# Text keys of the semantic scores copied on chip, and the second entry's scores ahead of slot 0

## The chip, the cores and the metric

The kernel runs on one core of one Trainium2 chip. The metric is the device time of one launch in microseconds. A run is compared by the median of its executions, and one further execution is recorded by the hardware profiler. The views quoted below come from that recorded execution.

## What is computed

Two cross-attention layers follow each other over 16 batch entries of 256 positions and 320 channels, with 20 heads of 16 channels. Both take the same context of 16 x 256 x 512. In layer 0 the first 77 context rows are text and the other 179 are image tokens; in layer 1 the last 4 rows are image tokens. The change touches layer 0 alone, and there the part that the reference writes as

```python
text_probs = softmax(einsum('bqc,bkc->bqk', q, k_text) * scale)   # over all channels, no heads
q_sem = einsum('bqk,bkc->bqc', text_probs, text)
sem = einsum('bqc,bnc->bqn', q_sem, ip) * scale
fused = scores + 0.5 * sem[:, None]                                # scores: per head, q x ip keys
ip_probs = softmax(fused) * spatial_mask
out = (text_out + ip_out) @ Wout + bout + x
```

The text keys `k_text` are thus needed twice: by head, in the attention itself, and over all 320 channels at once, in the semantic scores.

## The kernel before

**Numbers and splitting.** All products are made in a rounded 32-bit format. A value that needs more precision is held as a high part, rounded by ScalarE, and a low part, the difference, made by `halves` (line 148 holds the subtraction, line 147 the copy). A product of two such values takes three matmuls (`prod`, line 205).

**Slots.** Layer 0 is worked through in 80 slots, one for each entry and group of four heads, five groups to an entry; layer 1 follows with 80 more. `slot0(k)` writes one slot's order out by hand: the transposed maxima of slot k+1 (`maxima0`, matmul at line 657, then a copy and four small DMAs at line 661 into rows of `qs`), two rounds of score matmuls for slot k+2 (`score0`, line 649, with VectorE's row maxima at 650 and 651), two rounds of transposed scores for slot k (`turned0`, line 673, with the exponential on ScalarE at 676 and a product with `rs` on GpSimd at 679), the weighted values of slot k-1 (`attend0`, line 709, then `settle0`, lines 720 to 727), and `stacks(k + 4)`, DMAs that lay queries, keys and semantic rows of slot k+4 into `qs` and `ks`. PE's order is exactly the order of these calls. Before slot 0 a hand-written start-up, `begin`, fixes the order on every engine; after it, PE alone is fixed and the other queues are ordered by the compiler's scheduler.

**Tasks.** What an entry or a pair of entries needs besides is a generator with a list of due times in slots; `fill(now)` steps the earliest ones due. Those that matter here:

- `k0` c, the keys of entries 2c and 2c+1 (`keys0`; for pair 0 `keys_first`). It loads the pair's context (`context`, four 256 KB DMAs and four splittings, the low halves on GpSimd where the load is spread over slots), multiplies by the text and the image key weights for each of three blocks of 128 channels, splits the result into `kst`, a ring of two, and writes it to the DRAM tensor `kd` (`keys_out`).
- `q0` b, the queries, kept on chip as `qh` and written to `qd`.
- `m0t` b, the products of text and context rows; `v0` b, the values.
- `s0` b, the semantic scores (`semantic0`), in seven steps: fetch the text keys `kt`; two steps of six matmuls each of `qh` with `kt` (line 571) and their row maxima (573 to 578); exponentials (582); their normalisation (586); transposition (590) and splitting into `tph`; product with `m0t` (599, 600) and the exponential `rs`.

**Text keys.** `kt` lies in the buffer `kb`, of which there is one. For entry 0 `keys_first` fills it by three GpSimd copies from `kst` (line 331). For each of the other 15 entries the first step of `s0` issues two DMAs on SP's queue that read `kd` back, 144 KB each. In layer 1 `image1` uses `kb` for something else.

**The order at the start.** `s0` 1 takes its first step at the end of `begin`, which queues its two DMAs on SP ahead of the maxima of slot 1 and ahead of the context loads of `k0` 1. Its matmuls stand on PE at the end of slot 0, its transposition at the end of slot 1, its last product in slot 2. Because `stacks(5)`, the first of entry 1, needs `tph` of entry 1, slot 1 has no call of `stacks` and slot 2 has two. `s0` 2 fetches its keys in slot 2 and has its matmuls on PE in slot 3.

Of the kernel before, what the change touches and what calls it, by code (L numbers as in the profile page):

```python
# [9 lines left out]
FR = mybir.dt.float32r  # L10
# [7 lines left out]
S = 256  # L18
# [5 lines left out]
T0 = 77  # L24
# [14 lines left out]
LEAD = 4  # L39
# [9 lines left out]
def xattn2(  # L49
# [27 lines left out]
    nc = tc.nc  # L77
    f = lambda ap: ap.bitcast(F32)
    mm = nc.tensor.matmul

    def dma(out, in_):
        nc.sync.dma_start(*(f(ap) if ap.dtype == FR else ap for ap in (out, in_)))
# [11 lines left out]
        return ps.tile([128, 1024], F32, tag="S", name="S", bufs=1).rearrange("p (h t) -> p h t", h=4)  # L94


    words, slots = {"ctb": 1024, "cta": 1024, "raw": 512, "rawc": 512, "kb": 768, "si": 256, "mt": S, "mx": 2, "kst": 4 * S, "rs": 2 * S, "P": 4 * S}, {}

    def buf(tag, shape, dtype=F32, bufs=1, name=None):
        if tag in ("wB", "wD", "vr", "raw"):  # L100
# [108 lines left out]
    def context(b, n, wait=0):  # L209

        tiles, parts = [], []
        for k in range(0, 4, 3 - n):
            src = cT_d[:, b * S : (b + n) * S].rearrange("(k p) t -> p k t", p=128)[:, k : k + 3 - n]
            ct = buf("cta" if n == 1 or k < 2 else "ctb", [128, 2, 512], FR, bufs=SIZES["CTA" if n == 1 or k < 2 else "CTB"], name="ct")
            split = lambda t: t.rearrange("p (k t) -> p k t", t=n * S)
            parts.append((src, split(ct[:, 0]), split(ct[:, 1])))
            tiles.append(ct)
        yield from in_turn(parts, wait, "rawc raw" if b == 2 and n == 2 else "rawc", nc.gpsimd if wait else nc.vector)
        if n == 2:
            return lambda s, k: tiles[k][:, s].rearrange("p (b t) -> p b t", b=2)  # L220
        return lambda s, k: tiles[k // 2][:, s, (k % 2) * S : (k % 2 + 1) * S]
# [68 lines left out]
    def keys_out(d, m, kst, b=slice(None)):  # L290

        rows = slice(m * 128, (m + 1) * 128)
        for r, s in ((slice(0, 2), 0), (slice(2, 3), 1)):
            src = kst[:, s, b].rearrange("p b t -> p (b t)").unsqueeze(1)
            dma(d[r, rows, b].rearrange("r p b t -> p r (b t)"), src.to_broadcast([128, r.stop - r.start, src.shape[2]]))

    def keys0(c):
        if c not in ct0:
            tiles = context(2 * c, 2, 0.25)
            yield next(tiles)  # L300
            get("v0", 2 * c - 1)
            get("m0t", 2 * c - 1)
            ct0[c] = yield from tiles
        ct = ct0[c]
        for m in range(3):
            ms = slice(m * 128, (m + 1) * 128)
            kst = buf("kst", [128, 2, 2, S], FR, bufs=SIZES["KST"])
            for w, lo, hi, a, z in ((wk0, 0, 96, 0, T0), (wki0, T0 - 1, S, T0, S)):
                kp = bank()[:, : 2 * (hi - lo)].rearrange("p (b t) -> p b t", b=2)
                prod(kp, lambda s, k: w(s, k, ms), lambda s, k: ct(s, k)[:, :, lo:hi], 4)  # L310
                halves(kst[:, 0, :, a:z], kst[:, 1, :, a:z], kp[:, :, a - lo : z - lo])
                if a:
                    keys_out(kd[0][c], m, kst)
                yield

    def keys_first():

        ct = ct0[0]
        kst = [buf("kst", [128, 2, 2, S], FR, bufs=SIZES["KST"]) for i in range(2)]
        kst.append(buf("ho", [128, 5 * S], FR)[:, : 4 * S].rearrange("p (s b t) -> p s b t", s=2, b=2))  # L320
        kt = buf("kb", [128, 3, 2, 96], FR, name="kt")
        for w, lo, hi, a, z in ((wk0, 0, 96, 0, 96), (wki0, T0 - 1, S, T0, S)):
            for m in range(3):
                ms = slice(m * 128, (m + 1) * 128)
                kp = bank()[:, : 2 * (hi - lo)].rearrange("p (b t) -> p b t", b=2)
                prod(kp, lambda s, k: w(s, k, ms), lambda s, k: ct(s, k)[:, :, lo:hi], 4)
                halves(kst[m][:, 0, :, a:z], kst[m][:, 1, :, a:z], kp[:, :, a - lo : z - lo])
                if a:
                    keys_out(kd[0][0], m, kst[m], slice(0, 1))
                else:  # L330
                    nc.gpsimd.tensor_copy(kt[:, m], f(kst[m][:, :, 0, :96]))
                yield kt
        for m in range(3):
            keys_out(kd[0][0], m, kst[m], slice(1, 2))
        yield kt

    def values0_(b):
        ct, i = ct0[b // 2], b % 2
# [215 lines left out]
    def semantic0(b):  # L554

        qh, qd = get("q0", b)
        NT = 96
        kt = first_kt[0] if b == 0 else buf("kb", [128, 3, 2, NT], FR, name="kt")
        for s, r in ((0, 0), (1, 2)) if b else ():
            dma(kt[:, :, s], kd[0][b // 2, r].rearrange("(m p) b t -> p m b t", p=128)[:, :, b % 2, :NT])  # L560
        yield
        mh = get("m0t", b)

        tps = []
        for t in range(2):
            sf = bank()
            for k in range(3):
                qt = lambda h: qh[:, h, k, t * 128 : (t + 1) * 128]
                for h in range(2):
                    both = kt[:, k].rearrange("p s n -> p (s n)")  # L570
                    mm(sf[:, : 2 * NT], qt(h), both, start=k + h == 0, stop=k + h == 3)
            sp = buf("sp", [128, T0], bufs=2)
            nc.scalar.copy(sp, sf[:, NT : NT + T0])
            nc.vector.tensor_add(sp, sp, sf[:, :T0])
            mz = buf("mx", [128, 2], bufs=2)
            mx, zs = mz[:, 0:1], mz[:, 1:2]
            nc.vector.tensor_reduce(mx, sp, axis=AX.X, op=ALU.max)
            nc.vector.tensor_scalar_mul(mx, mx, -SCALE)
            tps.append((sp, mx, sp, zs))
            yield  # L580
        for sp, mx, tp, zs in tps:
            nc.scalar.activation(tp, sp, AF.Exp, bias=mx, scale=SCALE, accum_out=zs)
        yield
        for sp, mx, tp, zs in tps:
            nc.vector.reciprocal(zs, zs)
            nc.vector.tensor_scalar_mul(tp, tp, zs)
        yield
        tpp = bank()
        for t in range(2):
            nc.tensor.transpose(tpp[:T0, t * 128 : (t + 1) * 128], tps[t][2], ident)  # L590
        tph = buf("tph", [T0, 2, S], FR, bufs=2)
        nc.scalar.copy(tph[:, 0], tpp[:T0, :S])
        nc.vector.tensor_sub(tph[:, 1], tpp[:T0, :S], f(tph[:, 0]))
        yield

        rs = buf("rs", [128, 2, S], bufs=2)
        rp = bank().rearrange("p (t q) -> p t q", t=2)
        for t in range(2):
            mm(rp[:, t], mh[:, 0, t * 128 : (t + 1) * 128], tph[:, 1], start=True, stop=False)
            mm(rp[:, t], mh[:, 1, t * 128 : (t + 1) * 128], tph[:, 0], start=False, stop=True)  # L600
        nc.scalar.activation(rs, rp, AF.Exp, scale=SCALE)
        yield
        return qd, tph, rs, mh


    QK, P, W, R = {}, {}, {}, {}
# [81 lines left out]
    def slot0(k):  # L688
        if k > 0:
            yield lambda: maxima(k + 1)  # L690
        yield lambda: ahead(k + 2, 0)
        yield lambda: turned0(k, 0)
        yield 0.2
        if k == 2:
            yield lambda: stacks(k + LEAD - 1)
        if k > 0:
            yield lambda: attend0(k - 1)
        yield lambda: ahead(k + 2, 1)
        yield lambda: turned0(k, 1)
        if k != 1:  # L700
            yield lambda: stacks(k + LEAD)
        yield 0.6
        yield 1.0

# [257 lines left out]
    def task(key, times, make, *needs):  # L962
        tasks[key] = [times, 0, make, needs, len(tasks)]
# [38 lines left out]
    def shifted(n, *times):  # L1002

        return [RAMP(n + t) for t in times]

    first_kt, resid0 = [], []

    def first_keys():
        for kt in keys_first():
            if not first_kt:  # L1010
                first_kt.append(kt)
            yield

    FIRST = {"k0": [-1, 0.2, 0.6, 0.6, 1, 1.2, 1.6, 1.6, 2, 2.2, 2.6], "s0": [-1, 0.6, 1, 1.2, 1.6, 1.6, 2.2]}
    for c in range(B // 2):
        n, k = 10 * c, [("k0", c)] if c else []
        task(("k0", c), FIRST["k0"] if c == 1 else shifted(n, -14.4, -13.3, -13, -12.4, -12, -10.8, -10.4, -9.8, -9.4, -8.8, -8.4), (lambda c=c: keys0(c)) if c else first_keys,
             *([("w4", 0)] if c > 1 else []))
        task(("q0", 2 * c), shifted(n, -11.8, -11, -10, -9, -8), lambda b=2 * c: queries0(b))
        task(("q0", 2 * c + 1), shifted(n, -4.4, -4, -3, -2.8, -2), lambda b=2 * c + 1: queries0(b))  # L1020
# [26 lines left out]
    def stacks(k):  # L1047
        if 0 <= k < 2 * NS:
            (stacks0 if k < NS else stacks1)(k)
# [11 lines left out]
    def begin():  # L1061
# [25 lines left out]
        score0(1, 0)  # L1087
        stacks0(3)
        score0(1, 1)
        parts(("s0", 1))  # L1090
        maxima0(1, nc.sync)
        parts(("k0", 1))
        resid0.append(load(xT_d[0], "xc"))
        dma(mk, mk_d)
        dma(bo[:, 0, :], bo0_d)
# [95 lines left out]
```

## Time and profile before

| | |
|---|---|
| median of 3 runs | 1643.64 us (1639.58 to 1647.11) |
| the profiled execution | 1646.73 us, of which 1644.9 us from the first to the last instruction |
| mean granted TensorE clock | 0.972 |
| busy: PE, VectorE, ScalarE, GpSimd | 1539.0, 1197.1, 830.3, 1184.0 us |
| DMA, mean over the span | 150 GB/s |

Layer 0 takes about the first 650 us of the span, at some 8.2 us a slot. Times in the views are microseconds from the start of the span. In the timeline a row is a group of like instructions: start, length, engine, line, operation, output and input tile, shapes, count, and in brackets how long the engine had stood idle before it and what ended that. "PEld" is TensorE's weight load. A row of the stretches gives the length, then the busy time of PE, PEld, DVE, ACT and POOL with counts, the granted TensorE clock, the DMA share and the rate.

### The profile page before, as it was taken

To read this page: it belongs to the slowest core of one execution; us is meant where nothing else is said; L and a number is where in the kernel's file an instruction comes from. 1 tells how busy PE (TensorE), PEld (TensorE's weight loads), DVE (VectorE), ACT (ScalarE), POOL (GpSimd) and SP (SyncE) were. 2 spreads that over 40 slices of the span, in tenths; PEclk is the share of its full clock that TensorE was granted. 3 is DMA by queue.
4 is the path that set the end of the run, shared out by engine and by line. 5 is a ranking of instruction groups with operands and counts; after the bars stand their busy time and mean duration, and the time that the engine had idled before them with its cause. 6 is when DMAs were issued, how large, how long until landed. Compare 5 with 4: busy or idle time off the path is not lost.

```text
span 1644.9 us, 36268 instructions
## 1 busy us (share of the span) xinstructions
PE 1539.0 (94%) x13306; PEld 1239.6 (75%) x13306; DVE 1197.1 (73%) x2404; ACT 830.3 (50%) x1797; POOL 1184.0 (72%) x1131
## 2 busy tenths in 40 slices
PE   7789999999999899689999999999999999999996
PEld 6677878787878787577777777777777777777765
DVE  5467777677666677867777787778777887787685
ACT  5335445445454545435555455545555555555462
POOL 3358787868686867767687767767776787678675
PEclk9799999999999999789999999999999999999998
DMA  7766777777777676565324333343334233423301
GB/s 220 203 207 197 219 202 218 202 210 196 207 198 222 180 213 172 162 198 179 121 86 132 119 104 108 124 127 97 115 118 133 88 123 110 142 82 106 109 26 44
DMA packets 247742, 247.49 MB, mean 150 GB/s; under 512 B 31050, under 2 KB 231468, under 8 KB 247564
## 3 DMA queue, kind: packets, MB, share of 16 engines
q1 hardware_dynamic: 245356, 243.87, 50.1%
q8 instruction: 106, 1.74, 0.5%
q10 hardware_dynamic: 2208, 1.30, 0.3%
q14 instruction: 72, 0.59, 0.1%
HBM read 121.21 MB, written 88.18 MB: 127 GB/s over the span
## 4 chain that ended last, share of the span: by engine, by line
PE 54%; DVE 14%; DMA 10%; POOL 9%; ACT 5%; issue 4%; SPq 2%; ACTq 0%; POOLq 0%; DVEq 0%
PE X L205 16%; PE X L814 10%; PE X L522 7%; PE P L709 5%; POOL wt L805 4%; PE S L649 3%; PE P L823 3%; PE T L673 3%; DMA qs<-qd 3%; PE P L826 3%; PE T L775 2%; DMA qs<-mt 2%; DVE ho L512 2%; DMA kd<-kst 2%; DVE wt L815 2%
## 5 line engine op out<-in xcount | busy, mean ns | idle before, releaser
L679 POOL TENSOR_TENSOR P<-P,rs 128x512 f32<-128x512 f32 x320 | 412.6, 1310 | 171.3 <-ACT P L676 170.9
L805 POOL TENSOR_TENSOR wt<-P,ctb 128x512 f32<-128x512 f32 x320 | 422.4, 1335 | 117.1 <-ACT ctb L804 115.9
L814 PE MATMUL X<-ctb,gm 128*128 128x512 f32 x1120 | 328.8, 412 | 2.5 <-DVE wt L815 2.5
L676 ACT ACTIVATE P<-T 128x512 f32<-128x512 f32 x320 | 176.2, 595 | 234.5 <-PE T L673 118.4
L786 ACT ACTIVATE P<-T 128x512 f32<-128x512 f32 x320 | 174.1, 597 | 142.4 <-PE T L775 121.8
L815 DVE TENSOR_TENSOR wt<-X,wt 128x512 f32<-128x512 f32 x320 | 216.7, 679 | 25.7 <-PE X L814 23.0
L804 ACT ACTIVATE ctb<-P 128x512 fp32r<-128x512 f32 x320 | 195.8, 631 | 74.9 <-PE X L814 63.2
L814 PEld LDWEIGHTS X<-ctb,gm 128*128 128x128 f32 x1120 | 188.8, 188 | 49.4 <-DVE wt L815 5.2
L781 DVE TENSOR_REDUCE mn<-S 128x4 fp32r<-128x1008 f32 x160 | 191.1, 1194 | 0.6 <-PE S L780 0.6
L651 DVE TENSOR_REDUCE mn<-S 128x4 fp32r<-128x716 f32 x160 | 142.6, 891 | 0.0
L673 PE MATMUL T<-qs,ks 127*128 127x256 f32 x640 | 112.6, 296 | 22.9 <-DVE tmp L726 9.8
L649 PE MATMUL S<-ks,qs 125*128 125x256 f32 x640 | 119.1, 310 | 11.2 <-DVE mn L651 3.5
L709 PE MATMUL P<-P,vr 128*32 128x256 f32 x1920 | 128.9, 404 | 0.0
L649 PEld LDWEIGHTS S<-ks,qs 125*128 125x128 f32 x640 | 89.9, 197 | 48.3 <-issue 38.3
L522 PE MATMUL X<-ho,wF 128*128 128x256 f32 x768 | 112.9, 290 | 7.1 <-DVE ho L512 3.0
L894 POOL TENSOR_TENSOR r<-u,rs 128x40 f32<-128x40 f32 (+2 forms) x17 | 108.7, 6393 | 14.8 <-DVE u L891 14.7
L522 PE MATMUL X<-hq,wE 128*128 128x256 f32 x768 | 110.7, 288 | 6.6 <-POOL hq L512 3.1
L673 PEld LDWEIGHTS T<-qs,ks 127*128 127x128 f32 x640 | 93.3, 199 | 28.0 <-DVE tmp L726 11.7
L522 PEld LDWEIGHTS X<-ho,wF 128*128 128x128 f32 x768 | 103.6, 195 | 12.8 <-DVE ho L512 4.7
L522 PEld LDWEIGHTS X<-hq,wE 128*128 128x128 f32 x768 | 102.9, 194 | 11.0 <-POOL hq L512 3.8
L205 PE MATMUL X<-cta,wA 128*128 128x252 f32 (+1 forms) x720 | 100.9, 287 | 7.7 <-ACT wA L147 5.8
L650 DVE TENSOR_REDUCE mn<-S 128x4 fp32r<-128x308 f32 x160 | 74.8, 468 | 44.8 <-PE S L649 44.2
(196 smaller groups left out, 2814.9 us busy)
## 6 DMA issues: line engine op xcount, KB each, us to landing
qd<-q SPq DMA_DIRECT2D x96, 384.0 KB
qs<-tph SPq DMA_DIRECT2D x64, 308.0 KB
kd<-kst SPq DMA_DIRECT2D x73, 256.0 KB
rawc<-in_cT_dram SPq DMA_DIRECT2D x60, 256.0 KB
qs<-qd SPq DMA_DIRECT2D x80, 192.0 KB
ks<-kd SPq DMA_DIRECT2D x80, 192.0 KB
ks<-kd SPq DMA_DIRECT2D x160, 96.0 KB
qs<-qd SPq DMA_DIRECT2D x160, 96.0 KB
```

The source lines that it names most:

```text
L205: last = mm(out, lhs(a, k), rhs(b, k), start=i == 0, stop=i == len(terms) - 1)
L522: mm(pp, w(s, k, slice(m * 128, (m + 1) * 128)), a[:, t], start=i == 0, stop=i == len(terms) - 1)
L649: mm(sp[:, h], Q[: XROW + T0, h, t * 128 : (t + 1) * 128], K[: XROW + T0, h], start=True, stop=True)
L673: mm(st[p][:, j], K[:KS0, 2 * p + j, t * 128 : (t + 1) * 128], Q[:KS0, 2 * p + j], start=True, stop=True)
L676: exp = anchor(nc.scalar.activation(pt, st[p], AF.Exp, scale=SCALE))
L679: anchor(nc.gpsimd.tensor_mul(pt, pt, rs[:, t : t + 1].to_broadcast([128, 2, S])))
L709: mm(pv[32 * s : 32 * s + 32, o : o + S], v[:, vt, h : h + 32], P[k, s // 2][:, t, s % 2], start=vt < 2, stop=vt != 1,)
L781: anchor(nc.vector.tensor_reduce(maxes[k + 2][:, t], sp[:, :, :T1], axis=AX.X, op=ALU.max))
L804: nc.scalar.activation(R[k, u][:, t], P[k, u][:, t], AF.Copy, scale=0.5)
L805: anchor(nc.gpsimd.tensor_sub(W[k, u][:, t], P[k, u][:, t], f(R[k, u][:, t])))
L814: mm(yp, gm[:, gb], R[k, u][:, kt], start=i == 0, stop=i == len(blocks[n]) - 1)
L815: nc.vector.tensor_mul(W[k, u][:, n], yp, W[k, u][:, n])
```

## The change

- `kt` now holds both entries of a pair, 128 x 3 x 2 x 2 x 96 words, and `kb` grows from 768 to 1152 words.
- `keys0` fills it for every pair: after each splitting of a block of text keys, GpSimd copies 2 x 2 x 77 words a partition from `kst` into it. The 30 DMAs from `kd` to `kb` are gone; the first step of `s0` only picks its entry's part. `keys_first` clears the buffer once and copies both entries of pair 0.
- The matmul of line 571 reads two runs of 96 words that no longer lie side by side; its size stays.
- `s0` 1 moves ahead: `begin` makes its fetching step and its twelve matmuls before the maxima of slot 1 and its exponentials and normalisation after them, and its last two steps are due in slot 0 at 0.2 and 0.6. On PE the twelve matmuls therefore stand before the maxima of slot 1, the transposition between the two rounds of slot 0, the last product at slot 0's end.
- With that, `stacks(k + LEAD)` is called in every slot: `stacks(5)` in slot 1 and not in slot 2.
- The low halves of the context of pair 1 are made by VectorE, not GpSimd. They stand in VectorE's queue between the row maxima of slots 2 and 3 and after them.

```diff
@@ context
-        yield from in_turn(parts, wait, "rawc raw" if b == 2 and n == 2 else "rawc", nc.gpsimd if wait else nc.vector)
+        yield from in_turn(parts, wait, "rawc raw" if b == 2 and n == 2 else "rawc", nc.gpsimd if wait and b != 2 else nc.vector)
@@ keys0
         ct = ct0[c]
+        kt = kts[c] = buf("kb", [128, 3, 2, 2, 96], FR, name="kt")
         for m in range(3):
...
                 if a:
                     keys_out(kd[0][c], m, kst)
+                else:
+                    nc.gpsimd.tensor_copy(kt[:, m, :, :, :T0], f(kst[:, :, :, :T0]))
                 yield
@@ keys_first
-        kt = buf("kb", [128, 3, 2, 96], FR, name="kt")
-        for w, lo, hi, a, z in ((wk0, 0, 96, 0, 96), (wki0, T0 - 1, S, T0, S)):
+        kt = kts[0] = buf("kb", [128, 3, 2, 2, 96], FR, name="kt")
+        nc.gpsimd.memset(f(kt), 0.0)
+        for w, lo, hi, a, z in ((wk0, 0, 96, 0, T0), (wki0, T0 - 1, S, T0, S)):
...
-                    nc.gpsimd.tensor_copy(kt[:, m], f(kst[m][:, :, 0, :96]))
+                    nc.gpsimd.tensor_copy(kt[:, m, :, :, :T0], f(kst[m][:, :, :, :T0]))
@@ semantic0
-        kt = first_kt[0] if b == 0 else buf("kb", [128, 3, 2, NT], FR, name="kt")
-        for s, r in ((0, 0), (1, 2)) if b else ():
-            dma(kt[:, :, s], kd[0][b // 2, r].rearrange("(m p) b t -> p m b t", p=128)[:, :, b % 2, :NT])
+        kt = kts[b // 2][:, :, :, b % 2]
...
-                    both = kt[:, k].rearrange("p s n -> p (s n)")
-                    mm(sf[:, : 2 * NT], qt(h), both, start=k + h == 0, stop=k + h == 3)
+                    mm(sf[:, : 2 * NT].rearrange("p (s n) -> p s n", s=2), qt(h), kt[:, k], start=k + h == 0, stop=k + h == 3)
@@ slot0
-        if k == 2:
-            yield lambda: stacks(k + LEAD - 1)
...
-        if k != 1:
-            yield lambda: stacks(k + LEAD)
+        yield lambda: stacks(k + LEAD)
@@ due times of s0 for entry 1
-"s0": [-1, 0.6, 1, 1.2, 1.6, 1.6, 2.2]
+"s0": [-1, -1, -1, -1, -1, 0.2, 0.6]
@@ begin
-        parts(("s0", 1))
+        parts(*[("s0", 1)] * 3)
         maxima0(1, nc.sync)
-        parts(("k0", 1))
+        parts(("s0", 1), ("s0", 1), ("k0", 1))
```

More of the change, by code (lines that the diff above doesn't have):

```diff
@@ L94, in scores @@
         return ps.tile([128, 1024], F32, tag="S", name="S", bufs=1).rearrange("p (h t) -> p h t", h=4)
-    words, slots = {"ctb": 1024, "cta": 1024, "raw": 512, "rawc": 512, "kb": 768, "si": 256, "mt": S, "mx": 2, "kst": 4 * S, "rs": 2 * S, "P": 4 * S}, {}
+    words, slots = {"ctb": 1024, "cta": 1024, "raw": 512, "rawc": 512, "kb": 1152, "si": 256, "mt": S, "mx": 2, "kst": 4 * S, "rs": 2 * S, "P": 4 * S}, {}
     def buf(tag, shape, dtype=F32, bufs=1, name=None):
@@ L295, in keys_out @@
             dma(d[r, rows, b].rearrange("r p b t -> p r (b t)"), src.to_broadcast([128, r.stop - r.start, src.shape[2]]))
+    kts = {}
     def keys0(c):
@@ L330, in keys_first @@
                 else:
-                    nc.gpsimd.tensor_copy(kt[:, m], f(kst[m][:, :, 0, :96]))
-                yield kt
+                    nc.gpsimd.tensor_copy(kt[:, m, :, :, :T0], f(kst[m][:, :, :, :T0]))
+                yield
         for m in range(3):
             keys_out(kd[0][0], m, kst[m], slice(1, 2))
-        yield kt
+        yield
     def values0_(b):
@@ L1004, in shifted @@
         return [RAMP(n + t) for t in times]
[L1006 to L1014, printed above, removed]
+    resid0 = []
+    FIRST = {"k0": [-1, 0.2, 0.6, 0.6, 1, 1.2, 1.6, 1.6, 2, 2.2, 2.6], "s0": [-1, -1, -1, -1, -1, 0.2, 0.6]}
     for c in range(B // 2):
         n, k = 10 * c, [("k0", c)] if c else []
-        task(("k0", c), FIRST["k0"] if c == 1 else shifted(n, -14.4, -13.3, -13, -12.4, -12, -10.8, -10.4, -9.8, -9.4, -8.8, -8.4), (lambda c=c: keys0(c)) if c else first_keys,
+        task(("k0", c), FIRST["k0"] if c == 1 else shifted(n, -14.4, -13.3, -13, -12.4, -12, -10.8, -10.4, -9.8, -9.4, -8.8, -8.4), (lambda c=c: keys0(c)) if c else keys_first,
              *([("w4", 0)] if c > 1 else []))
```

## The prediction

> **What bounds the kernel now.** I read the page first: PE is busy for 94% of the span, no other engine above 73%, so over most of it time is PE's own work, and a wait counts if PE stands in it. Then PE's waits, longest in total first.
>
> ```profile
> PE X L571 <- DMA kb<-kd: 10.8, 2, 5.6
> PE T L673 <- DVE tmp L726: 9.8, 2, 5.9
> PE T L673 <- DMA qs<-mt: 8.9, 11, 1.3
> PE X L657 <- DVE mn L651: 7.5, 7, 2.9
> ```
>
> The first line is the transfer that the change removes: of 15 entries only two make PE wait for it, 10.8 us in all. The timeline shows both places.
>
> ```profile
> 58.68 1.05 PE L673 MATMUL T<-qs,ks 127*128 127x256 f32 x4
> 65.30 2.85 PE L571 MATMUL X<-kb,q 128*128 128x192 f32 x12 [5.57 <-DMA kb<-kd]
> 72.18 0.58 PE L205 MATMUL X<-ctb,wA 128*128 128x192 f32 x3 [0.63 <-POOL ctb L148]
> 74.12 2.23 PE L709 MATMUL P<-P,vr 128*32 128x256 f32 x24
> 107.35 2.84 PE L571 MATMUL X<-kb,q 128*128 128x192 f32 x12 [5.23 <-DMA kb<-kd]
> 112.15 1.55 PE L709 MATMUL P<-P,vr 128*32 128x256 f32 x24
> ```
>
> Place A is the end of slot 0 (entry 1), place B the end of slot 3 (entry 2). Entry 0's same twelve matmuls took 1.50 at 24.94, so after both waits they run at half speed. The stretches give the clock (the last three figures of a row are the granted clock, the DMA share and GB/s):
>
> ```profile
> 54.30:57.70 3.40, 1.43 (x11) 1.13 (x10) 2.23 (x4) 1.45 (x3) 0.53 (x1) 1.00 0.89 296
> 57.70:71.10 13.40, 7.83 (x36) 7.54 (x37) 2.46 (x8) 3.39 (x8) 7.22 (x7) 0.50 0.89 227
> 104.90:111.70 6.80, 4.35 (x21) 4.35 (x22) 2.52 (x11) 2.24 (x7) 2.91 (x3) 0.54 0.71 188
> ```
>
> PE was already slow from 57.7, before wait A. At A the DMA engines are loaded (0.89), so what was queued decides as well as what is waited for.
>
> **The change part by part.** The sum is made against the profiled execution, 1646.73 us; the median of the runs, 1643.64, lies 3.1 lower, and the predicted time is taken from the median. Gains are read at the next point that cannot move freely: PE's L709 at 74.12 for A and at 112.15 for B.
>
> *Place A.* The order on SP between slot 0's stacks and the context loads was two kb DMAs (59.65, 2.27 us of issue), the maxima of slot 1 (62.01, 2.52), then rawc at 64.58 and raw at 65.50. Without kb these start 2.27 earlier, on DMA engines with 288 KB less to move (at the stretch's 227 GB/s, 1.3 us). PE ends the first key block when the last context quarter has landed (ScalarE's copy at 71.71), is rounded (0.62) and subtracted. I let landing move by 3.0: more than issue alone, less than issue and bytes together (2.3 to 3.5; nothing if the queue ahead alone decides). The subtraction takes 1.27 on GpSimd; on VectorE ctb<-raw took 0.69 with GpSimd quiet, and the like L512 on VectorE averages 1.38 beside a busy GpSimd, so -0.6 to +0.1; I take -0.5, as GpSimd's products of slot 1 wait for ScalarE then. The semantic work itself does not vanish: its twelve matmuls go into the 0.90 and 0.97 gaps before slot 0's maxima (54.10, 55.30), the transposition (0.15 start to start at 78.16) and the last product (0.49 at 87.15) leave slots 1 and 2. That is 0.6 more. A: 3.0 + 0.5 + 0.6 = 4.1, from 0.6 to 8.2 (all of 59.73 to 67.95).
>
> The change adds one wait here. PE's queue is in order, and the transposition (L590) now stands between slot 0's rounds, behind the chain of L574, L577, L582, L586. VectorE has the maxima of slot 1 until 55.24, then this chain and slot 2's maxima (56.26 to 57.54 before) in turn; with rows of 0.23, 0.23, 0.15, ScalarE 0.36 and 0.19, and L586 at 0.27 to 1.33, it ends near 59.5 to 60. So the second round (57.69 before) starts some 2 us late, and queued behind it are slot 2's second maxima, slot 1's first round and the key block. That is cover, not cost: the key block waits for context until about 70 anyway. Without that cover it would cost those 2 us.
>
> *Place B.* The last kd write lands at 103.34 and kb 3.87 later. With GpSimd copies PE goes on at 102.1. Next late are the maxima of slot 5 (VectorE's L651, from 104.22 for 0.89), the small DMAs of slot 4 on ScalarE's queue (102.72 to 104.87) and GpSimd's products for slot 3 (105.65, 2.49, end 108.14), on which L709 depends. So L709 starts near 108.2 instead of 112.15: 3.9. stacks(7), queued on SP behind kb until 105.36, goes out earlier. Bounds: 2.2, if the clock halves for one window of 3.4 us here (1.7 lost), and 4.7, if only VectorE's maxima were late (110.0 to about 105.3).
>
> Which? Between 102.1 and 108.2 PE would be busy for 2.8 us, 46%. The first stretch above was 42% busy (1.43 of 3.40), its longest gap 1.0, and the clock was 0.50 after it: by this row the halving is possible. The Trainium skill ("TensorE: Matmul & The Clock Gate", the part on oscillation) says that what throttles is an idle gap over about 3.4 us; by it B keeps all 3.9, as its gaps stay shorter. The row differs from the rule, so I keep the loss in the range; I take 3.9 because windows do not line up with the gap.
>
> *GpSimd.* 21 copies of 128x308 are added after pair 0. The row nearest is L331, 128x192, 0.34 to 0.64; by size 0.55 to 1.0, I take 0.6: 12.6 us in all, bounds 0 and 21 on the path. PE's list shows no wait of layer 0's L709 for GpSimd, and GpSimd itself stood idle 171 us before L679, 2.1 a slot. At 321.86, where a first copy would fall, it had been idle 3.14. I cost the copies at nothing; uncovered they cost 12.6. The memset of kb (1152 words; 0.95 for 1024) and pair 0's longer copies lie in GpSimd's 2.08 idle before 13.28, or before L571's 24.94: nothing.
>
> The skill has a rule against this part ("SBUF — State Buffer", "Who interferes with whom"): GpSimd and VectorE share a port pair as a lock. The trace agrees: L586 took 0.27 at 28.15 with GpSimd quiet and 1.33 at 74.86 beside its products. If each copy held VectorE up by its own 0.6, the sum would be the 12.6 above again.
>
> *SP, DMA, the rest.* 28 further kb DMAs go, 144 KB each, in 384 rows each: 11,520 of 247,742 packets with A's. PE's waits for qs and ks transfers sum to 17.2 (8.9 for T, 7.1 for S, 1.2 for L657); a tenth of them, 1.5, is taken (0 to 4). stacks(5) goes from slot 2 to slot 1, four DMAs ahead of their need in slot 3: nothing. The strided key operand: 192 columns as before, 0.26 to 0.50 a matmul; no row shows two runs; nothing, at most 0.03 x 192 = 6 if each took a tenth longer; a gain is excluded by the equal column count.
>
> Sum: 4.1 + 3.9 + 1.5 = 9.5 us, 1637.2 for the profiled execution, 1634.1 for the median, -0.6%.
>
> **Rivals.** (1) The waits are handed on: context at A lands no sooner (DMA share 0.89 speaks for it), the clock halves at B, nothing comes of the lighter queue: 0.6 + 0.5 + 2.2 = 3.3, 1640.3. Against it: the 2.27 us of SP issue stand directly ahead of the loads. (2) More goes than read: A's wait whole (8.2), B 4.7, and 1.5: 14.4, 1629.2. For it: PE alone bounds what follows; against it: the context loads still end near 69. (3) Slower: the copies block GpSimd's queue. A copy must wait for its block's low half on VectorE; where the scheduler puts it ahead of products already due, L679 and then ScalarE's P buffers and PE's T wait. At 1.0 a copy and 1.0 of waiting, 21 times, 42 us land on GpSimd; it decides from the point where a copy's slot has less than the 2.1 us of average idle, and if half of that reaches PE the result is 9.5 - 21 = 11.5 slower, 1655. For it: GpSimd is busy 433 of 600 us between 40 and 640, and above 18 of 20 around 130; against it, the list without one such wait. That the change doesn't do what it says: the instruction order shows no DMA into kb any more.
>
> **How the numbers follow.** A difference under 0.5% (8.2 us) cannot be told from none here. The forecast has 0.5, rival 1 0.25, rival 2 0.13, rival 3 0.12. The forecast's own range is 1630 to 1638; its part above 1635.4 (1643.64 less 8.2), 0.08 of the 0.5, counts as the same, so 0.42 and rival 2's 0.13 make 0.55 faster, 0.08 and rival 1's 0.25 make 0.33 the same, rival 3 0.12 slower. The range takes in rival 2's 1629 with 3 us for the clock windows (half clock appeared at five places between 313 and 620, 3.4 or 6.8 us each), and above it all of rival 1: 1626 to 1646; rival 3 lies outside.
>
> **What would show it.** Right: no wait of PE for kb, L709's first group near 70 and its fourth near 104 (108.2 less A), context subtractions on VectorE near 0.7, no L709 wait for GpSimd. Wrong: PE waiting at L590 longer than context needs, L205 of the key block still ending near 74, copies of over 1 us or preceded by idle GpSimd with L679 behind them, L571 longer than 0.28.

## The result, and the profile after

The changed kernel takes 1630.48 us, the median of 5 runs (1626.80 to 1633.39); the kernel before, beside it, 1647.11 us (1639.58 to 1649.44). The ratio is 0.9909 with a 95% interval of 0.9880 to 0.9939. A second build of the same source (after_again, below) gave 1631.86 us and 0.9903 (0.9880 to 0.9927). The profiled execution of the changed kernel took 1630.48 us too, with a span of 1628.7 us against 1644.9 before: 16.2 us less, where the prediction's sum was 9.5.

The page of the changed kernel:

```profile
span 1628.7 us, 36230 instructions
PE 1533.9 (94%) x13306; PEld 1232.8 (76%) x13306; DVE 1209.1 (74%) x2410; ACT 830.2 (51%) x1797; POOL 1189.4 (73%) x1147
DMA packets 235741, 243.06 MB, mean 149 GB/s; under 512 B 19050, under 2 KB 219468, under 8 KB 235564
```

GpSimd is busy 5.4 us longer than before (1184.0): the copies, less the context halves it no longer makes. PE's share is the same. PE's waits, longest in total first (us in total, times, longest):

```profile
PE T L676 <- DMA qs<-mt: 10.2, 13, 1.4
PE T L676 <- DVE tmp L726: 9.9, 2, 5.9
PE X L660 <- DVE mn L654: 8.5, 7, 2.9
```

Line numbers are 3 higher than before in this part of the code (L571 is now L574, L590 L593, L673 L676); L709 and L720 to L727 stay. The wait for the keys' transfer, 10.8 us and first of the list before, is gone; the three lines behind it are still there, 0.1 to 1.3 us longer.

**Where the 16 us came from.** The start of a slot is read as the first of its T matmuls (L673, now L676). Times between such starts, in us, from the two profiled executions:

| slots | before | after | gain |
|---|---|---|---|
| start to slot 0 | 56.1 | 55.7 | 0.4 |
| 0 to 5 (places A and B) | 62.8 | 60.0 | 2.8 |
| 5 to 50 | 373.4 | 366.9 | 6.5 |
| 50 to 76 | 232.0 | 230.1 | 1.9 |
| 76 to 79 (end of layer 0) | 28.6 | 23.8 | 4.8 |

These sum to 16.4 and come from one execution of each kernel; layer 1 runs alike in both to within some tenths. So the places for which the prediction had 8.0 gave 2.8, the middle for which it had 1.5 gave 6.5, and 4.8 came from a place that it did not name.

**Place A**, rows of VectorE, ScalarE and PE in the timeline of after, in order of time:

```profile
59.39 0.49 PE L593 MATMUL X<-ident,sp 128*77 128x128 f32 x1 [0.66 <-DVE sp L589]
67.84 0.68 DVE L148 TENSOR_TENSOR cta<-rawc,cta 128x512 fp32r<-128x512 f32 x1
68.44 1.76 DVE L148 TENSOR_TENSOR ctb<-raw,ctb 128x512 fp32r<-128x512 f32 x1
70.08 0.62 ACT L147 CAST ctb<-raw 128x512 fp32r<-128x512 f32 x1 [1.34 <-DMA raw<-in_cT_dram]
70.73 1.15 DVE L148 TENSOR_TENSOR ctb<-raw,ctb 128x512 fp32r<-128x512 f32 x1 [0.53 <-ACT ctb L147]
72.61 2.79 PE L709 MATMUL P<-P,vr 128*32 128x256 f32 x24
```

The semantic chain has ended by 59.39, just ahead of the predicted 59.5 to 60. But the last quarter of the context is copied at 70.08, only 1.6 us sooner than before (71.71), and L709 starts at 72.61, 1.5 sooner. The stretches beside it show why even this is not all kept (the last three figures are the granted clock, the DMA share and GB/s):

```profile
54.30:57.70 3.40, 1.40 (x9) 1.10 (x9) 2.99 (x11) 2.09 (x7) 0.90 (x1) 0.91 0.91 305
57.70:61.10 3.40, 2.17 (x9) 1.91 (x10) 2.34 (x5) 0.65 (x3) 1.58 (x2) 0.50 0.97 203
67.90:71.30 3.40, 1.98 (x6) 1.50 (x6) 2.87 (x4) 1.46 (x3) 2.96 (x2) 0.50 1.05 206
71.30:74.70 3.40, 2.76 (x22) 1.49 (x26) 0.90 (x2) 0.29 (x1) 0.20 (x2) 0.50 0.31 83
```

PE has only 1.98 us of work in the stretch before L709, and the half clock lasts through it: 20.5 us in one piece from 57.1, where before had 17.1 us in two pieces between 57 and 79. So L709 takes 2.79 instead of 2.23.

**Place B**, PE's rows and two stretches:

```profile
100.12 1.48 PE L574 MATMUL X<-kb,q 128*128 128x192 f32 x12
103.16 0.23 PE L660 MATMUL X<-ident_r,mn 128*8 128x128 f32 x1 [1.50 <-DVE mn L654]
106.77 2.79 PE L709 MATMUL P<-P,vr 128*32 128x256 f32 x24 [2.20 <-DVE mx L581]
109.48 1.22 PE L652 MATMUL S<-ks,qs 125*128 125x256 f32 x4
101.50:104.90 3.40, 1.56 (x11) 1.10 (x9) 3.40 (x10) 1.84 (x6) 1.94 (x2) 0.99 0.73 240
104.90:108.30 3.40, 1.53 (x16) 0.91 (x20) 2.87 (x11) 1.73 (x6) 3.40 (x4) 0.50 0.93 233
```

The twelve matmuls take 1.48 instead of 2.84 and wait for nothing. L709 starts 5.4 us sooner than before. But the clock has halved at 104.9, for 6.8 us: L709 takes 2.79 where it took 1.55, and of the 7.2 us that slot 4 leads by, 3.2 are left at slot 5.

**The copies** of GpSimd, and the first T matmuls of slot 76's second half, before and after:

```profile
74.53 0.44 POOL L318 CAST kb<-kst 128x308 fp32r<-128x308 f32 x1 [3.20 <-DVE kst L148]
732.01 0.77 PE L673 MATMUL T<-qs,ks 127*128 127x256 f32 x2 [2.24 <-DVE P L724]
717.59 0.63 PE L676 MATMUL T<-qs,ks 127*128 127x256 f32 x4
```

Of the 21 copies 17 take 0.44 to 0.45 us and four 0.91 to 0.92. Nine of them come after idle time of GpSimd, the others directly behind its other work. Three times (3.9 us in all) the profile has ScalarE's exponential wait for one, and no L709 does. At slot 76 the kernel before waits 2.24 us for VectorE's work on the value tile P; after, the same matmuls wait for nothing. The change touches nothing there. These matmuls read nothing of P, so the wait points to a PSUM bank in which the compiler has put both tiles, before and not after; the trace shows the wait and not the bank.

### The profile page after: what moved, and what is told of

It reads as the page before. It is cut to its first block, busy times and chain, and to the rows that moved or that the text cites. A ratio compares the mean times of both kernels' runs of the same rounds, so it can differ in the third digit from the quotient of the medians.

```text
span 1628.7 us, 36230 instructions
## 1 busy us (share of the span) xinstructions
PE 1533.9 (94%) x13306; PEld 1232.8 (76%) x13306; DVE 1209.1 (74%) x2410; ACT 830.2 (51%) x1797; POOL 1189.4 (73%) x1147
## 4 chain that ended last, share of the span: by engine, by line
PE 52%; DVE 15%; POOL 11%; DMA 9%; ACT 6%; issue 4%; SPq 2%; ACTq 0%; POOLq 0%; DVEq 0%
PE X L205 15%; PE X L814 9%; PE X L528 7%; PE P L709 5%; POOL wt L805 4%; PE S L652 3%; POOL P L682 3%; PE P L823 3%; DMA qs<-qd 3%; PE P L826 2%; PE T L676 2%; PE T L775 2%; DVE wt L815 2%; DMA kd<-kst 2%; DVE mn L781 2%
## 5 line engine op out<-in xcount | busy, mean ns | idle before, releaser
L676 PE MATMUL T<-qs,ks 127*128 127x256 f32 x640 | 112.1, 295 | 22.0 <-DMA qs<-mt 10.2
L709 PE MATMUL P<-P,vr 128*32 128x256 f32 x1920 | 129.4, 404 | 2.2 <-DVE mx L581 2.2
L676 PEld LDWEIGHTS T<-qs,ks 127*128 127x128 f32 x640 | 92.8, 198 | 27.0 <-DVE tmp L726 11.6
L205 PEld LDWEIGHTS X<-cta,wA 128*128 128x128 f32 x720 | 93.8, 194 | 15.2 <-ACT wA L147 6.5
```

The costliest lines, as they stand in the source:

```text
L205: last = mm(out, lhs(a, k), rhs(b, k), start=i == 0, stop=i == len(terms) - 1)
L676: mm(st[p][:, j], K[:KS0, 2 * p + j, t * 128 : (t + 1) * 128], Q[:KS0, 2 * p + j], start=True, stop=True)
L709: mm(pv[32 * s : 32 * s + 32, o : o + S], v[:, vt, h : h + 32], P[k, s // 2][:, t, s % 2], start=vt < 2, stop=vt != 1,)
```

## The experiments

Each kernel was profiled once and timed in 5 rounds with the kernel before; the ratio is to before. A table at the end of the section has the stretches of all.

**after_again and spare_loads** ask whether the 28 transfers taken from SP's queue carry the gain. after_again is the changed kernel, built again. spare_loads puts the 28 back at their old step, into a tile that nothing reads:

```diff
         kt = kts[b // 2][:, :, :, b % 2]
+        for s, r in ((0, 0), (1, 2)) if b > 1 else ():
+            dma(spare[:, :, s], kd[0][b // 2, r].rearrange("(m p) b t -> p m b t", p=128)[:, :, b % 2, :NT])
```

> The changed kernel once more, unchanged, as the yardstick for the others of this group. In its first profile the two places of the prediction gave only 3.2 us by slot 5; 7.8 us came between slots 25 and 50 and 4.9 at slot 76, where nothing of the change stands ahead of PE. If those two stretches come from the change (loads gone, or queues in another order), the drift against the kernel before has the same shape in this profile, about 10 us by slot 50 and 16 by slot 77, and the time is again 15 us lower (1627 to 1634). If they are the luck of where half-clock windows fall, the shape differs by several us in these stretches.

> The changed kernel plus the 28 loads of text keys for entries 2 to 15, issued on SP where they were before, into a buffer that nothing reads. Theory load (the 28 loads in the DMA queues held up the small transfers that PE waits for): most of the later gain is lost again, 1638 to 1643. Theory order (the gain lies in the order of the queues, or in the clock, not in the bytes): no change beyond 3 us against the changed kernel, 1628 to 1634. My prediction's own price for the loads, 1.5 us, gives 1632.

after_again: 1631.86 us, and the gain has the same shape as in the first profile: 10.1 us ahead of the kernel before at slot 50, where after is 9.7 ahead. Up to slot 5 it is 4.2 instead of 3.2, behind slot 76 2.5 instead of 4.8, so a stretch of one execution can be off by 2 us. spare_loads: 1643.58 us, ratio 0.9982 (0.9966 to 0.9998). The transfers alone, with nobody waiting for their data, take back 11.7 us, and the stretch of slots 5 to 50 grows from 367 to 381 us. PE's waits for S, the scores, and SP's own wait, between 120 and 485 us, first in spare_loads, then in before, then in after:

```profile
PE S L655 <- DMA qs<-qd: 5.1, 8, 1.4
PE S L655 <- DMA qs<-mt: 2.2, 2, 1.3
SPq L82 <- DMA spare<-kd: 10.8, 4, 3.7
...
PE S L649 <- DMA qs<-mt: 2.8, 3, 1.2
PE S L649 <- DMA qs<-qd: 2.4, 3, 1.1
PE S L649 <- DMA ks<-kd: 0.9, 1, 0.9
...
PE S L652 <- DMA qs<-qd: 1.1, 3, 0.4
PE S L652 <- DMA qd<-q: 0.9, 1, 0.9
```

SP stands at the head of its queue until key rows have landed in device memory, and the stacks' transfers behind it come late for S. Half clock in slots 5 to 50: 20.5 us against 6.8 (after) and 13.7 (after_again).

**pair0_only** keeps the new start but reads the keys of entries 2 to 15 back, as before; **chip_old_order** takes the old start and order with all keys on chip.

```diff
@@ pair0_only, semantic0
-        kt = kts[b // 2][:, :, :, b % 2]
+        if b < 2:
+            kt = kts[0][:, :, :, b]
+        else:
+            kt = buf("kb", [128, 3, 2, NT], FR, name="kt")
+            for s, r in ((0, 0), (1, 2)):
+                dma(kt[:, :, s], kd[0][b // 2, r].rearrange("(m p) b t -> p m b t", p=128)[:, :, b % 2, :NT])
@@ chip_old_order: the kernel before, with the copies of keys0 and keys_first and kt = kts[b // 2][:, :, :, b % 2]
```

> The changed kernel with text keys on chip for entries 0 and 1 only; entries 2 to 15 read them back from DRAM by 28 loads as before, and GpSimd makes no copies after pair 0. So the start stays as changed. Theory load: the time goes to 1640 to 1645, since place B (5 us idle at entry 2) and the later gain both go. Theory order: place B's net 1.3 us are lost and little else, 1631 to 1636. If the copies cost anything on GpSimd, this kernel gains that back.

> The kernel before with text keys on chip for all entries, but entry 1's semantic scores at their old place, two calls of stacks in slot 2, and pair 1's context low halves on GpSimd (pair 0's keys lie in a buffer that is loaded with weights later). Both waits for the key loads are gone as in the changed kernel. If copying the keys is the whole change, 1628 to 1635. If the order around slot 0 matters, it lies between: by the start alone the wait of 5.6 us at slot 0 is replaced by the context wait, so 1632 to 1638.

pair0_only: 1644.48 us, 0.9987 (0.9969 to 1.0006), not to be told from before. chip_old_order: 1633.38 us, 0.9924 (0.9897 to 0.9950). Nearly the whole gain belongs to the keys of the later entries; the changed start by itself is worth 1.5 to 1.9 us by these medians, which cannot be told from nothing.

**spare_tiny and spare_ready** split what spare_loads adds. spare_tiny reads one word of each row (1/96 of the bytes, as many rows); spare_ready reads as many bytes of the context input, which is always there.

```diff
@@ spare_tiny
+            dma(spare[:, :, s, :1], kd[0][b // 2, r].rearrange("(m p) b t -> p m b t", p=128)[:, :, b % 2, :1])
@@ spare_ready
+            dma(spare[:, :, s], cT_d[:CP, b * S : b * S + NT].rearrange("(m p) t -> p m t", p=128))
```

> As spare_loads (the changed kernel plus the 28 loads into a buffer that nothing reads, which brought 11.7 us back), but each row of a load is one word instead of 96: the same place in SP's queue, the same wait for the keys in DRAM, the same 384 rows, and 1/96 of the bytes. If it is the bytes on the DMA engines, the loss goes: 1630 to 1634. If it is SP's queue (a wait and an issue ahead of the transfers of a slot's stacks), the loss stays: 1640 to 1645, with PE's score matmuls still waiting for qs.

> As spare_loads, with all its bytes, but the loads read an input that is there from the start instead of the keys just written, so they never hold SP's queue for a transfer to land. If the wait at the head of SP's queue is the cause, 1630 to 1634. If it is bytes, or the issue itself of about 1 us a pair of loads, 1638 to 1645.

spare_tiny: 1641.02 us, 0.9962 (0.9947 to 0.9978). Bytes are not it: about 9 of the 12 us stay with a hundredth of them, and SP still waits for kd ("spare<-kd" 12.7 us in four waits). spare_ready: 1644.10 us, 0.9987 (0.9971 to 1.0003), but this is no clean answer. With nothing to wait for, the compiler moved all 28 loads ahead, to between 11.6 and 116.5 us: slot 0 begins 5.5 us later, the middle keeps the gain (369.2 us), and the wait of slot 76 is back (29.5 us for the last stretch).

**spare_qh and spare_qh_half** leave small transfers in place and take the wait away: the source is the on-chip query tile. spare_qh has 28 of them, spare_qh_half 14.

```diff
@@ spare_qh
+        for s, r in ((0, 0), (1, 2)) if b > 1 else ():
+            dma(spare[:, :, s, :1], qh[:, s, :, :1])
@@ spare_qh_half
+        for s, r in ((0, 0),) if b > 1 else ():
```

> Twenty-eight transfers put back at the same step of the semantic scores as in spare_tiny, as small as there (4-byte rows), but read from the query tile on chip instead of the rows written to device memory: SP has no landing of a key write to wait for. Theory that the loss of about 10 us in spare_tiny came from SP waiting at the head of its queue for the keys' rows to land, with the stacks' transfers behind it: this one stays near the changed kernel, 1630 to 1635 us, stretch of slots 5 to 50 366 to 369 us, and TensorE's waits of S for qs<-qd stay near 1 us. Rival, that each further transfer on SP costs by itself (its issue, its lane, its descriptors): 1638 to 1643 us, stretch 375 to 380 us, with 4 us or more of such waits again.

> As spare_qh, with one of the two transfers for each entry from 2 on: 14 small reads of the query tile instead of 28; TensorE's order is that of spare_qh. Theory that each further transfer on SP has a price of its own (spare_qh lost 12 us for 28, 0.43 us each): half the loss, 1636 to 1639 us, stretch of slots 5 to 50 about 368 to 369 us. Rival, that spare_qh lost its time at two chance meetings outside the middle stretch (slots 50 to 53, 6.7 us, and 72 to 73, 6.7 us in its profile), which another placing of the transfers may miss: 1630 to 1634 us with these two stretches at 24 and 9 us as in the changed kernel; or, if both meet again, 1641 to 1645 us however few transfers there are.

spare_qh: 1643.41 us (1636.32 to 1648.49 in 12 runs), 0.9982 (0.9966 to 0.9999). spare_qh_half: 1639.09 us (1634.86 to 1643.60), 0.9961 (0.9946 to 0.9976). By the total the rival of a price for each transfer fits: 0, 14 and 28 of them give 1631.9, 1639.1 and 1643.4. By the place it does not, as far as one execution of each tells: SP's wait for the spare tile is down to 0.4 us, and slots 5 to 50 take 370.4 and 365.4 us, not 375 to 380. These two executions are the slowest (1648.49) and the fastest (1634.86) of their twelve, and the twelve of spare_qh_half fall into two groups, 1634.9 to 1636.9 and 1641.3 to 1643.6. In the profiles the loss stands elsewhere; spare_qh at slot 51 and slot 72, ScalarE's rows and PE's, then VectorE's and PE's:

```profile
489.52 1.09 ACT L682 ACTIVATE P<-T 128x512 f32<-128x512 f32 x2 [2.67 <-DMA xc<-in_xT_dram]
494.99 0.46 PE L663 MATMUL X<-ident_r,mn 128*8 128x128 f32 x2 [1.16 <-ACT P L682]
501.69 2.79 PE L712 MATMUL P<-P,vr 128*32 128x256 f32 x24
...
688.78 4.19 DVE L148 TENSOR_TENSOR wE<-rawc,wE 128x384 fp32r<-128x384 f32 x1
694.25 2.59 PE L529 MATMUL X<-ho,wF 128*128 128x256 f32 x8 [6.24 <-ACT ho L518]
```

By the profile ScalarE idles until a transfer that has nothing to do with its exponential has landed, its queue holding the small DMAs of the maxima; and a subtraction of layer 1's weights takes 4.19 us beside GpSimd's products (0.94 to 1.56 for those of the same shape in the changed kernel), with the transposition that PE needs behind it. Each is followed by half clock, 6.7 us lost at each place (30.6 against 23.9 us for slots 50 to 53, 15.2 against 8.5 for 72 to 73). spare_qh_half loses 2.7 and 4.2 us in the same two stretches. The second place cannot be charged to the transfers: slot 72 takes 11.3 to 13.5 us in six of the other kernels too, four of which have no added transfer (chip_old_order 12.8, ctx_gpsimd 11.3, copies_twice 13.4, early_ctx_late_rs 13.5). Slots 50 to 53 take 23.8 to 24.3 us in all kernels but these two.

So the middle is 8.5 to 11 us longer in the profiles with the wait at SP's head (378.9 and 381.3 against 370.4). PE stands idle there about as long in all three, 21.1 and 22.9 against 20.3 us; the rest is half clock, 20.5 us in both against 3.4, and that differs by 6.8 us between two executions of the changed kernel alone. In total 28 transfers without the wait cost 11.6 us, as much as with it. That the added transfers cost is shown; that the wait at the head of the queue is the reason, and not their number, is argued and not shown.

**copies_twice** doubles each of GpSimd's 21 later copies.

```diff
                     nc.gpsimd.tensor_copy(kt[:, m, :, :, :T0], f(kst[:, :, :, :T0]))
+                    nc.gpsimd.tensor_copy(again, f(kst[:, :, :, :T0]))
```

> Each of the 21 GpSimd copies of the text keys in the later entries is made a second time into a scratch tile: 21 x 0.44 = 9.2 us more on GpSimd, spread over the slots from 5 on. Theory that the copies cost nothing because GpSimd is idle there: 1629 to 1633 us, no line of PE waiting on GpSimd for the values. Rival 3 of the prediction, that the copies block the products behind them: half or more of the 9.2 us comes back, 1635 to 1640 us.

1640.38 us, 0.9966 (0.9949 to 0.9983): 8.5 us slower than the changed kernel for 9.2 us of copies, as the rival had it and not my theory. L711 (values) waits for GpSimd once, for 0.9 us at 728.79, long after the last copy. The profiled execution, 1646.44, is the slowest of its twelve. In slots 12 to 14 of it, which took 22.2 us against 15.1, GpSimd, VectorE, ScalarE and PE show the way:

```profile
171.51 0.44 POOL L319 CAST kb<-kst 128x308 fp32r<-128x308 f32 x1
171.90 0.44 POOL L320 CAST again<-kst 128x308 fp32r<-128x308 f32 x1
172.29 0.29 POOL L731 COPY hsn<-hsn 128x128 f32<-128x128 f32 x1
177.04 0.43 DVE L741 STREAM_TRANSPOSE hT<-hsn 128x256 f32<-128x256 f32 x1
179.90 0.83 ACT L519 CAST ho<-hT 128x768 fp32r<-128x768 f32 x1 [2.09 <-DMA ks<-kd]
180.78 2.59 PE L530 MATMUL X<-ho,wF 128*128 128x256 f32 x8 [4.61 <-ACT ho L519]
```

The small copy of the finished heads (L731) stands behind a pair of products and two copies; the work on the heads then stands behind VectorE's maxima until 177.04 and, on ScalarE, waits 2.09 us for a transfer. In the changed kernel that copy runs at 166.24, ahead of them, and PE's matmuls for wF at 174.91 wait for nothing. This stretch costs 7.1 us in its profile; another 4.9 go at slot 72, where no copy is near.

**ctx_gpsimd** gives the low halves of pair 1's context back to GpSimd.

```diff
-nc.gpsimd if wait and b != 2 else nc.vector
+nc.gpsimd if wait else nc.vector
```

> The changed kernel with the low halves of pair 1's context on GpSimd again. In the changed kernel VectorE's last two of these took 1.76 and 1.15 us beside GpSimd's products, not the 0.69 that I had taken, and GpSimd is idle before them. If this part of the change gives nothing, the same time within 3 us of the changed kernel and the first L709 group near 73; if GpSimd is the better place, 1 us sooner there; if it is worse, its four subtractions of 1.27 push the first products of slot 1 back by up to 5 us, and that group starts near 75.

1633.24 us, 0.9920 (0.9897 to 0.9943), against 1631.86: within what can be told. VectorE's halves gain 1.4 us by the medians, which cannot be told from nothing.

**early_ctx** issues the context loads of pair 1 in the start-up directly behind the first three stacks, ahead of the semantic step and the maxima.

```diff
-        parts(("s0", 1), ("s0", 1), ("k0", 1))
+        parts(("s0", 1), ("s0", 1))
@@ after stacks0(2)
-        parts(k0)
+        parts(k0, ("k0", 1))
```

> The changed kernel with the four context loads of pair 1 queued on SP in the start-up right after the stacks of slot 2, some 11 us sooner, instead of at its end. In the changed kernel PE's first key block ends only when the last of them has landed (70.1). If that landing sets the end of slots 0 and 1, the first L709 group starts 3 to 6 us sooner and the time falls by as much, to 1625 to 1629. If the semantic chain between slot 0's rounds or the maxima of slot 1 are as late, at most 1 us is gained.

1633.61 us, 0.9921 (0.9896 to 0.9946). Slot 2 starts 4.0 us sooner than in the changed kernel, the half clock between 57 and 79 is 10.2 us instead of 20.5, and the lead holds to slot 14; 1.5 us of it are left at slot 50 and 1.1 at slot 76. There the wait is back:

```profile
719.25 0.76 PE L676 MATMUL T<-qs,ks 127*128 127x256 f32 x2 [2.25 <-DVE P L724]
```

**early_ctx_late_rs** adds one shift, the last step of entry 1's semantic scores, after which, as the expectation has it, the compiler places the tiles of slot 76 in other banks.

```diff
-"s0": [-1, -1, -1, -1, -1, 0.2, 0.6]
+"s0": [-1, -1, -1, -1, -1, 0.2, 1.2]
```

> early_ctx (the context of entries 2 and 3 loaded right after the first three stacks) with one more shift: the last step of entry 1's semantic scores (the four products for rs) due 1.2 instead of 0.6 slots in, which the compiler answers with other PSUM banks: at slot 76 the second T tile waits for ScalarE and not for the value tile's reader on VectorE. Theory that early_ctx lost 4 to 5 us to that bank alone: stretch of slots 76 to 79 23 to 26 us instead of 29.1, the 4.0 us won by slot 2 kept to the end, total 1626 to 1630 us. Rival, that the early gain is eaten by the waits that follow whatever the bank: 1631 to 1634 us with the stretch at 23 to 26 us. If the stretch stays at 28 to 29 us, the bank is not its cause.

1629.66 us (1626.29 to 1630.08), 0.9897 (0.9878 to 0.9917). The wait is gone:

```profile
717.91 0.64 PE L676 MATMUL T<-qs,ks 127*128 127x256 f32 x4
```

The last stretch takes 23.2 us instead of 29.1, and the total is 4.0 us below early_ctx: the price of this wait, by the only pair of kernels that differ in little else (in the profiles slots 5 to 50 differ by 2.2 us too). It is the fastest median of all, but 1 to 2 us from the changed kernel, which the intervals cannot tell apart.

Stretches in us from the profiles (one execution each, whose own time stands beside the median of the runs):

| kernel | 0 to 5 | 5 to 50 | 50 to 76 | 76 to 79 | profiled | median |
|---|---|---|---|---|---|---|
| before | 62.8 | 373.4 | 232.0 | 28.6 | 1646.7 | 1647.1 |
| after | 60.0 | 366.9 | 230.1 | 23.8 | 1630.5 | 1630.5 |
| after_again | 57.8 | 367.6 | 230.5 | 26.1 | 1632.6 | 1631.9 |
| spare_loads | 55.4 | 381.3 | 231.1 | 23.1 | 1643.8 | 1643.6 |
| pair0_only | 61.9 | 373.1 | 229.7 | 29.5 | 1644.6 | 1644.5 |
| chip_old_order | 61.3 | 368.8 | 231.0 | 28.7 | 1639.7 | 1633.4 |
| spare_tiny | 59.2 | 378.9 | 229.5 | 23.7 | 1641.2 | 1641.0 |
| spare_ready | 60.8 | 369.2 | 229.5 | 29.5 | 1642.9 | 1644.1 |
| spare_qh | 59.7 | 370.4 | 242.5 | 26.0 | 1648.5 | 1643.4 |
| spare_qh_half | 57.6 | 365.4 | 236.0 | 25.7 | 1634.9 | 1639.1 |
| copies_twice | 60.2 | 376.7 | 232.3 | 25.9 | 1646.4 | 1640.4 |
| ctx_gpsimd | 60.9 | 366.8 | 230.9 | 23.9 | 1632.2 | 1633.2 |
| early_ctx | 54.4 | 369.3 | 230.5 | 29.1 | 1633.7 | 1633.6 |
| early_ctx_late_rs | 54.3 | 367.1 | 229.7 | 23.2 | 1626.3 | 1629.7 |

## Why the prediction was right or wrong

The direction and the range hold: 1630.5 in 1626 to 1646. The level is 3.6 us off, the difference 7.1 us: the median of before that the prediction started from, 1643.64 of three runs, is 1645.2 to 1647.1 in larger groups. The sum of 9.5 was made of terms that missed in both directions, and 4.8 us came from a place that no term names; that the time still falls in the range is in part luck.

- **Place A, 4.1: mis-sized.** It gave 1.5 by the row that the prediction chose. The step that failed is the landing of the context, 3.0 for 2.27 us of issue that vanish: the maxima's DMAs on SP took 2.99 instead of 2.52, the loads went out 1.9 us sooner (rawc at 62.66, raw at 63.61), and the last quarter was copied 1.6 sooner. The subtraction, taken at 0.69 because "GpSimd's products of slot 1 wait for ScalarE then", met them: 1.76 and 1.15 at 68.44 and 70.73, beside products at 68.34, while the two on cta took 0.68 and 0.69. The lock of which the Trainium skill speaks ("SBUF — State Buffer", "Who interferes with whom") fits these rows; by them, not the rule, the gain of 0.5 becomes nothing. The matmuls moved ahead cost nothing, as said; of the 0.6 that their leaving slots 1 and 2 was to give, 0.3 show, as the lead grows from 1.5 at L709 to 1.8 at slot 3. That the loads of slot 0 are the lever was right: early_ctx moves them and gets the 4.0.
- **Place B, 3.9: mis-sized, and the row that the prediction set aside was the right one.** L709 starts at 106.77; less A's lead of 1.8 at slot 3, B had given 3.5 by there, close to 3.9. But it had worked out 46% PE work ahead of L709, had a row with 42% and half clock after it, and took the whole 3.9 "because windows do not line up with the gap". Here PE was busy 1.56 of 3.40 us, its longest gap 1.5, and the clock went to 0.50 for 6.8 us. The step that failed is to read the gain at L709 as one that is kept: half clock behind it takes more than half of it back. Of B 1.3 are left at slot 5. The Trainium skill's rule ("TensorE: Matmul & The Clock Gate", on oscillation), no idle gaps over some 3.4 us, does not account for this row: the gap is shorter.
- **The lighter queue, 1.5 (0 to 4): mis-sized, and the largest single term.** It gave 6.5 in slots 5 to 50. The prediction took a tenth of PE's waits for qs and ks. The waits of S alone fell from 6.1 to 2.0 us in 120 to 485, and the prediction did not price the half clock, of which slots 5 to 50 have 13.7 us before, 6.8 after and 13.7 in after_again. All PE's idle time there is 19.9, 16.4 and 13.8 us. With half of the half clock counted as lost, the gain is an estimated 3.5 of waits and 3.4 of clock in after (6.5 measured) and 6.1 of waits alone in after_again (5.8 measured): its size repeats, its split does not. The prediction also called the transfers a matter of bytes and packets; spare_tiny shows that it is not the bytes. Whether SP's wait for kd or the number of transfers makes it stays open.
- **GpSimd's copies at nothing: right in this kernel, and less safe than it was put.** Most took 0.44, four 0.91, against 0.55 to 1.0 estimated, and no L709 waits for them. The doubled copies show that the cover is thin: rival 3's mechanism, a queue behind the copies, is real, but the item that mattered in slots 12 to 14 was not the products: it was the copy of the finished heads.
- **Slot 76, 4.8, not foreseen.** No step of the prediction could give it: it comes with a wait for the value tile that the compiler's placing of tiles may explain. The five kernels with this wait take 28.6 to 29.5 us for the last stretch, the others 23.1 to 26.1.
- **Rivals.** Rival 1's half clock at B and late landing at A both came, and its price for them (0.6 + 0.5 + 2.2) is near the measured 2.8; it was wrong in that nothing comes of the queue. Rival 2's time, 1629.2, is nearest the result, but for other reasons: neither place gave its whole wait.

## What to carry to other kernels

Take transfers off a busy DMA queue if their reader can have the data on chip: these 28 were worth some 12 us, though only one of their 14 entries made PE wait for its own keys. When a stretch of PE would be under half busy, cost the work behind it at half clock. And look at what a change moves at places that it does not touch: a wait at slot 76 and the order of small instructions were here worth as much as a planned step.

## What was not expected of the hardware

- The clock halves without a long gap: at place B after 1.56 us of work in 3.40 with gaps of at most 1.5 us. Cut into pieces of 3.41 us that begin where the clock changes, before and after have 21 pieces at full clock with PE busy for less than half, and half clock follows each of them; it follows none with PE busy for more than 0.6. At the start it stayed at 0.50 for 20.5 us while PE was 58 to 87% busy in most stretches.
- 28 transfers of 4-byte rows on SP cost nearly what 28 of full rows do: 9.2 against 11.7 us; with an on-chip source they cost 11.6.
- In spare_qh VectorE's subtraction of 128x384 took 4.19 us at 688.78, while GpSimd's products ran, and 0.51 at 693.26, when they had ended.
